# Convolution over 1563 fixed tiles of the sorted edge list, in chunks of 30, with a read base node and the radial attributes loaded by row

## The chip, the core and the metric

The program runs on one core of a Trainium2 chip. The metric is the time on the device in microseconds (us): the median of three runs of the whole program. The engines of the core are named PE (matmul; PEld is its weight load), DVE (vector), ACT (scalar), POOL and SP. POOL issues the gathers, SP most of the other DMAs. Each engine works through its own instructions in a fixed order and waits on semaphores for the others.

## What is computed

Two graph layers over 6250 nodes of 128 features and 200,000 edges that are sorted by their target `dst`. The first is a pair of attention layers with a residual; the change leaves it alone. The second is a convolution, and it is what the change is about:

```
h  = relu(layernorm(x))
f  = h @ W_lin_feat          # per node, 128 wide: 32 scalars, 32 vectors
s  = h @ W_lin_self
e  = f[src]                  # gathered per edge
w  = W_tp . gelu(gelu(edge_attr_8 @ W_mlp1) @ W_mlp2)   # 8 -> 64 -> 64 -> 4x32 per edge
m  = products of w, e and edge_attr_4 (a0, a1)          # 256 wide per edge
agg[dst] += m                # sum over the edges of a node
x  = x + cos * s + sin * (agg @ Wf)
```

(Scale factors are left out.)

## The kernel before

The program first runs the attention layers (to about 3030 us of the profiled execution), ending with `finish2`, which writes the node features `f` to a table in DRAM (`table3`) and leaves x + cos * s for all nodes in SBUF (`xt`). Then comes the convolution, written as one loop that is fully unrolled.

*Blocks and windows.* The nodes are cut into 49 blocks of 128. For each block, a window of 34 x 128 = 4352 edges of the sorted list is taken that starts at the block's first edge; that start is found on the chip and read into a register (`window_start`). An edge of the window that belongs to another block gets no place in the block's one-hot matrix and so adds nothing. A window has 34 tiles of 128 edges (K), worked on in groups of 8, 8, 8, 8 and 2 tiles (`GROUPS`): 245 groups, 1666 tiles.

*One group* (`convolve`). POOL issues one indirect DMA per tile that fetches 128 rows of `table3` (`gather`, L308) into one of six buffers `G`. PE transposes the group's radial attributes (L1165), ACT copies the result to SBUF as `a8t` (L1167), and PE multiplies it with a block-wise copy of `W_mlp1`, one matmul per pair of tiles (L1172). Two tiles of a pair share the 128 rows of the output, 64 hidden values each. ACT applies the first gelu (`hid1`, L1175), PE the second layer (L1177), ACT the second gelu (`hid2`, L1179), and PE the last product, one matmul per tile (L1185), into `big`. ACT scales the gathered rows by a0 (`g0`, L1196, one instruction per tile). DVE makes the products (L1198 to L1208). ACT and DVE split the results into a rounded half and its remainder (`halve`, L324 and L325), and DVE makes the one-hot matrices of the next group (`one_hot`, L317). At last PE adds each tile into the block's accumulator, a matmul with the one-hot matrix as its weights (the scatter, L1214). The accumulator is one PSUM bank (`whole`, a pool of one buffer).

*The end of a block.* ACT copies one half of the accumulator and DVE adds the other (`sums3`, L1244 and L1245). `finish3` transposes the sums on PE (L1224), ACT copies them (L1226), PE multiplies them with `Wf` (L1229), DVE adds the residual from `xt` (L1232, L1233), and SP stores 128 rows of the output (L1237).

*Order.* The code above is the order in which the work is written; a scheduler then sets each engine's order. It draws the front end of one group (L1165 to L1185) ahead of the scatter of the group before, so that PE works on two or three groups in turn. At a block's end, twelve of the next group's L1185 matmuls stand between the last scatter and the transposes of `finish3`.

After the loop stands a general path (`general3`) for lists that break the assumptions (too many edges in a window, or an unsorted list). A flag that is computed on the chip decides on it, and with these inputs it isn't taken.

Of the kernel before, what the change touches and what calls it, by code (L numbers as in the profile page):

```python
# [25 lines left out]
F32 = mybir.dt.float32  # L27
# [20 lines left out]
HS = 7  # L48
LAG = 5
# [12 lines left out]
def gnn_kernel(ctx: ExitStack, tc: tile.TileContext, x, src, dst, attr4, attr8,  # L62
               W1, al1, ar1, b1, W2, al2, ar2, b2,
               Wl0, Wl1, Ws0, Ws1, Wm1, Wm2, Wtp, Wf0, Wf1, out):
# [23 lines left out]
    NROW = (E - WCAP) // WSTEP + 1  # L88
    assert NB % HS == 0 and ROWT % WSEG == 0 and REST and HD == P // 2 and (E - WCAP) % WSTEP == 0

# [177 lines left out]
    srcw = const.tile([P, NB, K], I32, name="srcw")  # L268
    dstw = const.tile([P, NB, K], F32, name="dstw")
# [266 lines left out]
    table3 = dram.tile([NB * P, D], F32, name="table3")  # L536
    counts = [dram.tile([NQ, P, NB * QN], BF16, name=f"counts{b}") for b in range(NB)]
# [92 lines left out]
    wm1_sb = const.tile([SB * NRAD, NPR, 2 * HID], F32, name="wm1_sb")  # L630
    nc.vector.memset(wm1_sb, 0.0)
    for c in range(SB):
        nc.scalar.dma_start(wm1_sb[c * NRAD:(c + 1) * NRAD, c % NPR, c // NPR * HID:(c // NPR + 1) * HID], Wm1)
# [392 lines left out]
    xt = ctx.enter_context(tc.tile_pool(name="xt", bufs=1)).tile([P, NB, D], F32, name="xt")  # L1026

# [7 lines left out]
    with tc.tile_pool(name="att2", bufs=1) as pool, tc.tile_pool(name="dense", bufs=2) as dense, \  # L1035
# [8 lines left out]
        def finish2(b0, n):  # L1044
# [44 lines left out]
            nc.sync.dma_start(rows_of(table3, b0, n), t3[:, :n, :])  # L1089

# [3 lines left out]
        for b0 in range(0, NB, 2):  # L1094
# [8 lines left out]
            acc = big().rearrange("p (k a) c -> p k (a c)", k=2)  # L1103
            for h0 in range(0, NB, HS):
# [55 lines left out]
    def convolve(G, n, a0, a1, a8, acc, start, stop, oh, then=None):  # L1160
# [3 lines left out]
        pa = small()  # L1164
        nc.tensor.transpose(pa[:n * NRAD, :P], a8.rearrange("p c r -> p (c r)"), ident)  # L1165
        a8t = cw.tile([SB * NRAD, P], F32, name="a8t")
        nc.scalar.copy(a8t[:n * NRAD, :], pa[:n * NRAD, :P])  # L1167

        npr = min(n, NPR)
        ph = small()  # L1170
        for j in range(npr):
            nc.tensor.matmul(ph[:, j * P:(j + 1) * P], wm1_sb[:n * NRAD, j, :], a8t[:n * NRAD, :],  # L1172
                             start=True, stop=True)
# [39 lines left out]
        for c in range(n):  # L1213
            nc.tensor.matmul(acc, oh[:, c, :], ms[:, c].rearrange("e s h i u -> e (s h i u)"),  # L1214
                             start=start and c == 0, stop=stop and c == n - 1)
# [4 lines left out]
    def finish3(a, b, n):  # L1220
# [9 lines left out]
        o = cw.tile([P, D], F32, name="o")  # L1230
        xb = xt[:, ds(b, 1), :].rearrange("p o f -> p (o f)")
# [5 lines left out]
        nc.sync.dma_start(out[ds(b * P, n), :], o[:n, :])  # L1237

    with tc.tile_pool(name="conv", bufs=1) as pool, tc.tile_pool(name="gath3", bufs=6) as gath:
        again, some = flags(pool, over)  # L1240

# [6 lines left out]
        groups = [(b, *g) for b in range(NB) for g in GROUPS]  # L1248

        def hots(i):  # L1250
            b, s, n = groups[i]
            return one_hot(dstw[:, b, s:s + n], n)

        oh = hots(0)
        for i, (b, s, n) in enumerate(groups):
            if s == 0:
                r = window_start(b)
                a4 = cw.tile([P, K, 4], F32, name="a4", bufs=3)
                nc.sync.dma_start(a4, attr4[ds(r, CAP), :].rearrange("(p k) f -> p k f", p=P))
                a8 = cw.tile([P, K, NRAD], F32, name="a8", bufs=3)  # L1260
                nc.sync.dma_start(a8, attr8[ds(r, CAP), :].rearrange("(p k) f -> p k f", p=P))
                acc = whole()
                a1 = kept[:, P + b % 2 * 3 * K:P + (b % 2 + 1) * 3 * K].rearrange("p (k f) -> p k f", f=3)
                nc.vector.tensor_copy(a1, a4[:, :, 1:])
            cs = slice(s, s + n)
            G = gath.tile([P, SB, D], F32, tag="G", name="G")
            gather(G, table3, srcw[:, b, cs], n)
            oh = convolve(G, n, a4[:, cs, 0:1], a1[:, cs, :], a8[:, cs, :], acc, s == 0, s + n == K, oh,
                          (lambda i=i: hots(i + 1)) if i + 1 < len(groups) else None)
            if b and s == 0:  # L1270
                finish3(done, b - 1, P)
            if s + n == K:
                done = sums3(acc)
        finish3(done, FULL, REST)
# [4 lines left out]
        def general3(b, n):  # L1279
            with tc.If(flag_of(again[0:1, ds(b, 1)]) > 0):  # L1280
                nc.vector.tensor_copy(base, starts[:, ds(b, 1)])
                nc.vector.memset(tot3, 0.0)
                with tc.For_i(0, NCHUNK, 1) as i:
                    si, di = load_chunk(i)
                    dl = work.tile([P, GK], F32, name="dl")
                    nc.vector.tensor_scalar(dl, di, base, None, op0=OP.subtract)
                    at = []
                    for f, attr in ((4, attr4), (NRAD, attr8)):
                        t = cw.tile([P, GK, f], F32, name=f"a{f}g")
                        nc.vector.memset(t, 0.0)  # L1290
                        nc.sync.dma_start(t[:GP], attr[ds(i * (GP * GK), GP * GK), :].rearrange(
                            "(p k) f -> p k f", p=GP))
                        at.append(t)
# [40 lines left out]
```

## Time and profile before

| | us |
|---|---|
| median of three runs | 4724.91 |
| lowest, highest | 4715.71, 4729.55 |
| the profiled execution, its own time | 6136.95 |
| its span, first to last instruction | 6135.2 |

Busy time in the profiled execution, over the span:

| engine | busy us | share | instructions |
|---|---|---|---|
| PE | 3425.7 | 56% | 23441 |
| PEld | 2683.7 | 44% | 23442 |
| DVE | 3642.0 | 59% | 6107 |
| ACT | 2978.4 | 49% | 7370 |
| POOL | 2783.4 | 45% | 2787 |

The profiled execution is 30% longer than the timed ones; its durations of single instructions are used, and its waits have to be read with care. In the lines of the profile, a group is written as line, engine, operation, output<-inputs, shapes and count, then the busy time and the mean of one in ns, then the idle time of the engine just before these instructions and what ended it. "issue" is a wait for nothing that the profile shows, "remote" one that was ended from a queue it doesn't know. In the slices, each digit is a fortieth of the span, in tenths of busy time; PEclk is the granted clock of PE. In the order of time, a line has its start, its length, engine, line of code and operation.

### The profile page before, as it was taken

To read this page: it belongs to the slowest core of one execution; us is meant where nothing else is said; L and a number is where in the kernel's file an instruction comes from. 1 tells how busy PE (TensorE), PEld (TensorE's weight loads), DVE (VectorE), ACT (ScalarE), POOL (GpSimd) and SP (SyncE) were. 2 spreads that over 40 slices of the span, in tenths; PEclk is the share of its full clock that TensorE was granted. 3 is DMA by queue.
4 is the path that set the end of the run, shared out by engine and by line. 5 is a ranking of instruction groups with operands and counts; after the bars stand their busy time and mean duration, and the time that the engine had idled before them with its cause. 6 is when DMAs were issued, how large, how long until landed. Compare 5 with 4: busy or idle time off the path is not lost. (4 is left out here: it accounts for less than half of the span.)

```text
span 6135.2 us, 69889 instructions
## 1 busy us (share of the span) xinstructions
PE 3425.7 (56%) x23441; PEld 2683.7 (44%) x23442; DVE 3642.0 (59%) x6107; ACT 2978.4 (49%) x7370; POOL 2783.4 (45%) x2787
## 2 busy tenths in 40 slices
PE   3123555555555555799655555555655555655555
PEld 2013444454454444688534333333433333433333
DVE  4244655655665565788656565555655565556556
ACT  2012665665565566799634444334433433434434
POOL 1665545444544451000155555445555555545553
PEclk9999565666665566899867777667767667666667
DMA  3243434443443343444211111111111111111110
GB/s 86 63 115 85 119 111 115 117 115 111 125 123 113 108 129 122 171 163 154 89 42 42 40 40 41 38 40 40 42 41 42 40 41 41 39 38 42 39 40 25
DMA packets 338660, 480.00 MB, mean 78 GB/s; under 512 B 188987, under 2 KB 228555, under 8 KB 334306
## 3 DMA queue, kind: packets, MB, share of 16 engines
q1 hardware_dynamic: 186626, 232.52, 12.3%
q0 software_dynamic: 89072, 154.07, 10.7%
q10 hardware_dynamic: 62576, 88.69, 4.3%
q8 instruction: 191, 3.13, 0.2%
q14 instruction: 195, 1.60, 0.1%
HBM read 369.53 MB, written 105.48 MB: 77 GB/s over the span
## 5 line engine op out<-in xcount | busy, mean ns | idle before, releaser
L308 POOL DMA_INDIRECT G<-table,srcw x2720 | 2712.2, 997 | 2950.6 <-issue 989.7
L1214 PE MATMUL whole<-halves,ohr 128*128 128x512 f32 x1666 | 660.3, 556 | 255.6 <-DVE halves L325 228.1
L862 ACT ACTIVATE ramp<-erb,sel 128x256 bf16<-128x256 f32 x1764 | 758.4, 499 | 0.7 <-issue 0.3
L1177 PE MATMUL small<-hid,wm_sb 128*128 128x512 f32 (+1 forms) x490 | 335.3, 775 | 661.7 <-issue 467.2
L757 ACT CAST ca<-small 128x392 bf16<-128x392 f32 x784 | 349.3, 482 | 572.7 <-remote 383.5
L1214 PEld LDWEIGHTS whole<-halves,ohr 128*128 128x128 f32 x1666 | 433.9, 276 | 434.7 <-DVE halves L325 273.7
L325 DVE TENSOR_TENSOR halves<-mid,halves 128x1024 fp32r<-128x1024 f32 (+1 forms) x245 | 260.5, 1063 | 596.6 <-ACT halves L324 450.6
L1175 ACT ACTIVATE hid<-small 128x512 f32<-128x512 f32 (+1 forms) x245 | 135.6, 553 | 964.5 <-remote 579.4
L755 PE MATMUL small<-key,lo 128*128 128x98 bf16 x3136 | 333.5, 257 | 444.0 <-ACT ca L757 239.3
L1196 ACT ACTIVATE g<-G,a 128x128 f32<-128x128 f32 x1666 | 535.3, 394 | 17.9 <-DMA a<-in_edge_attr 8.3
L1185 PE MATMUL big<-wtp_sb,hid 64*128 64x128 f32 x3332 | 365.2, 356 | 221.7 <-issue 153.2
L1185 PEld LDWEIGHTS big<-wtp_sb,hid 64*128 64x128 f32 x3332 | 297.9, 247 | 412.3 <-issue 264.6
L1109 ACT ACTIVATE ramp<-small,sel 128x256 bf16<-128x256 f32 (+1 forms) x1225 | 447.8, 620 | 61.1 <-DVE up L1113 26.5
L755 PEld LDWEIGHTS <-lo 128*128 128x128 bf16 x3136 | 258.9, 127 | 481.6 <-issue 463.1
L325 DVE TENSOR_TENSOR halves<-big,halves 128x1024 fp32r<-128x1024 f32 (+1 forms) x245 | 259.3, 1058 | 354.2 <-ACT halves L324 175.9
L744 DVE TENSOR_TENSOR lo<-slots,turned 128x2048 bf16<-128x2048 bf16 x196 | 239.5, 1222 | 349.6 <-PE small L755 179.8
L1172 PE MATMUL small<-a8t,wm_sb 64*128 64x128 f32 (+1 forms) x1764 | 360.4, 355 | 96.4 <-issue 71.9
L882 PE MATMUL up<-rc,up 128*128 128x102 bf16 x3528 | 319.5, 264 | 165.9 <-DVE up L864 106.9
L1177 PEld LDWEIGHTS small<-hid,wm_sb 128*128 128x128 f32 x490 | 95.7, 241 | 719.5 <-issue 491.1
L1179 ACT ACTIVATE hid<-small 128x512 f32<-128x512 f32 (+1 forms) x245 | 135.8, 554 | 543.9 <-PE small L1177 284.1
L1172 PEld LDWEIGHTS small<-a8t,wm_sb 64*128 64x128 f32 (+1 forms) x1764 | 303.6, 251 | 169.9 <-issue 112.4
L370 PE MATMUL whole<-halves,ohr 128*128 128x136 f32 x1054 | 250.6, 387 | 218.3 <-issue 64.9
(273 smaller groups left out, 6596.2 us busy)
## 6 DMA issues: line engine op xcount, KB each, us to landing
counts<-ca ACTq DMA_DIRECT2D x196, 392.0 KB
ct<-counts SPq DMA_DIRECT2D x196, 392.0 KB
rc<-rhs SPq DMA_DIRECT2D x63, 717.5 KB
G<-table,srcw POOLq DMA_INDIRECT x2720
oht<-dlow SPq DMA_DIRECT2D x31, 1088.0 KB
ctc<-counts SPq DMA_DIRECT2D x504, 56.0 KB
a<-in_edge_attr SPq DMA_DIRECT2D x49, 136.0 KB
rhs<-rc SPq DMA_DIRECT2D x7, 717.5 KB
```

The costliest lines, as they stand in the source:

```text
L308: nc.gpsimd.indirect_dma_start(out=G[:, c, :], out_offset=None, in_=table, in_offset=bass.IndirectOffsetOnAxis(ap=idx[:, c:c + 1], axis=0))
L325: nc.vector.tensor_tensor(ms[1], m, ms[0], op=OP.subtract)
L755: nc.tensor.matmul(ps[:, k * NKEY:(k + 1) * NKEY], lo[:, a, :, r], ky[:, a, :, r], start=True, stop=True)
L757: nc.scalar.copy(ca[:, :, i * W:(i + WBANK) * W].rearrange("p h (k d) -> p h k d", d=W), ps[:, :WBANK * NKEY].rearrange("p (k h d) -> p h ...
L862: nc.scalar.activation(ramp[:, i, :n * P], erb[:, h, :n * P], AF.Relu, bias=sel1[:, h0 + i, h:h + 1], scale=STEEP)
L882: nc.tensor.matmul(ups[k][:, h], up[:, i, k * P:(k + 1) * P], by_head[:, i, :, h, :], start=h0 + i + h == 0, stop=h0 + i + h == NB + H1 - 2)
L1109: nc.scalar.activation(ramp[:, h, :n * P], pe[:, :n * P], AF.Relu, bias=sel2[:, h0 + h, :], scale=STEEP)
L1172: nc.tensor.matmul(ph[:, j * P:(j + 1) * P], wm1_sb[:n * NRAD, j, :], a8t[:n * NRAD, :], start=True, stop=True)
L1177: nc.tensor.matmul(ph[:, :npr * P], wm2_sb, hid1[:, :npr * P], start=True, stop=True)
L1185: nc.tensor.matmul(pw[:, c, :], hid2[half, j * P:(j + 1) * P], wtp_sb[half].rearrange("x p u -> x (p u)"), start=True, stop=True)
L1196: nc.scalar.activation(g0[:, c], G[:, c, :], AF.Copy, scale=a0[:, c, :])
L1214: nc.tensor.matmul(acc, oh[:, c, :], ms[:, c].rearrange("e s h i u -> e (s h i u)"), start=start and c == 0, stop=stop and c == n - 1)
```

## The change

The convolution no longer goes by blocks of nodes but by the edge list itself. The host cuts the list into 1563 tiles of 128 edges (the last one filled up) and hands it over as `src_tiles`, `dst_tiles`, `attr_4_tiles` and `attr_8_rows`, the last with one row per radial attribute. 195 groups have 8 tiles, one has 3.

The tiles are summed in 53 chunks of 30 (`CT`). A chunk has a base node, the target of its first edge, and its one-hot matrices count from there. `load_tiles`, called in the stage ahead of the convolution, reads the two lists, finds the bases, shifts `dst` by them and computes the flag for the general path (`again3`). At a chunk's end (`close`), which can fall within a group, the accumulator is read out as before. Since the next chunk's nodes overlap with it, its sums are carried over: `same`, a matrix that shifts rows by the difference of the bases, adds them into the next accumulator by one more matmul after six tiles. `finish3` then writes 128 rows at the base, and the next chunk overwrites those which it completes. Its residual rows come from a copy of `xt` in DRAM (`xtd`), loaded at the base, which SP reads from `base_i`.

For the first layer, the radial attributes are loaded by two DMAs per group straight into `a8t` (16 rows, 8 per half of the group, 512 columns; four buffers), so the transpose and the copy go, and one product of 512 columns takes the place of the four. `a4` is loaded for 40 tiles at a time.

```diff
+CT, LT = 30, 40
...
-    srcw = const.tile([P, NB, K], I32, name="srcw")
-    dstw = const.tile([P, NB, K], F32, name="dstw")
+    srcw = pool.tile([P, NB, K], I32, name="srcw")
+    dstw = pool.tile([P, NB, K], F32, name="dstw")
...
-    wm1_sb = const.tile([SB * NRAD, NPR, 2 * HID], F32, name="wm1_sb")
+    wm1_sb = const.tile([2 * NRAD, 2 * HID], F32, name="wm1_sb")
...
+    def load_tiles(pool):
+        nc.sync.dma_start(srcc, src_t)
+        raw = dstc.bitcast(I32)
+        nc.sync.dma_start(raw, dst_t)
+        firsts = pool.tile([1, NCH + 1], F32, name="firsts")
+        nc.vector.memset(firsts, N - 1.0)
+        nc.vector.tensor_copy(firsts[:, 1:NCH], raw[0:1, CT:NT:CT])
...
+        nc.vector.tensor_scalar(bd[:, 0, :], firsts[:, :NCH], float(N - P), None, op0=OP.min)
+        nc.vector.tensor_copy(base_i, bd[:, 0, :])
...
+        nc.vector.tensor_scalar(shift, ps[:, NCH:2 * NCH], -1.0, own, op0=OP.mult, op1=OP.add)
...
             nc.sync.dma_start(rows_of(table3, b0, n), t3[:, :n, :])
+            nc.sync.dma_start(rows_of(xtd, b0, n), xt[:, bs, :])
...
+            if b0 == 8:
+                load_tiles(pool)
...
-    def convolve(G, n, a0, a1, a8, acc, start, stop, oh, then=None):
-        pa = small()
-        nc.tensor.transpose(pa[:n * NRAD, :P], a8.rearrange("p c r -> p (c r)"), ident)
-        a8t = cw.tile([SB * NRAD, P], F32, name="a8t")
-        nc.scalar.copy(a8t[:n * NRAD, :], pa[:n * NRAD, :P])
+    def convolve(G, n, a0, a1, a8t, sink, oh, then=None):
         npr = min(n, NPR)
+        rows = NRAD if n <= NPR else 2 * NRAD
         ph = small()
-        for j in range(npr):
-            nc.tensor.matmul(ph[:, j * P:(j + 1) * P], wm1_sb[:n * NRAD, j, :], a8t[:n * NRAD, :],
-                             start=True, stop=True)
+        nc.tensor.matmul(ph[:, :npr * P], wm1_sb[:rows], a8t[:rows, :npr * P], start=True, stop=True)
...
         for c in range(n):
-            nc.tensor.matmul(acc, oh[:, c, :], ms[:, c].rearrange("e s h i u -> e (s h i u)"),
-                             start=start and c == 0, stop=stop and c == n - 1)
+            acc, start, stop = sink(c)
+            nc.tensor.matmul(acc, oh[:, c, :], ms[:, c].rearrange("e s h i u -> e (s h i u)"), start=start, stop=stop)
...
+        def close(c):
+            xb = cw.tile([P, D], F32, name="xb")
+            nc.sync.dma_start(xb, xtd[ds(first_node(c), P), :])
+            state["sums"] = sums3(state["acc"])
+            todo.append((c, state["sums"], xb))
+
+        def sink(t):
+            c, k = divmod(t, CT)
+            end = min(CT, NT - c * CT) - 1
+            if k == 0:
+                if c:
+                    close(c - 1)
+                state["acc"] = whole()
+            if k == min(6, end) and c:
+                same = cw.tile([P, P], F32, name="same")
+                nc.vector.tensor_scalar(same, slot, shift[:, c - 1:c], None, op0=OP.is_equal)
+                nc.tensor.matmul(state["acc"][:, :2 * D], same, state["sums"], start=False, stop=False)
+            return state["acc"], k == 0, k == end
...
+        for t in range(0, NT, SB):
+            n = min(SB, NT - t)
+            i = t // SB % (LT // SB)
+            if i == 0:
+                m = min(LT, NT - t)
+                a4 = cw.tile([P, LT, 4], F32, name="a4", bufs=3)
+                nc.sync.dma_start(a4[:, :m], attr4_t[:, t:t + m, :])
...
+            a8t = cw.tile([2 * NRAD, NPR * P], F32, name="a8t", bufs=4)
+            for j in range(2 if n > NPR else 1):
+                c = (t + j * NPR) * P
+                nc.sync.dma_start(a8t[j * NRAD:(j + 1) * NRAD, :], attr8_t[:, c:c + NPR * P])
...
+            gather(G, table3, srcc[:, t:t + n], n)
+            waiting = len(todo)
+            oh = convolve(G, n, a4[:, cs, 0:1], a1s[:, cs, :], a8t, lambda c: sink(t + c), oh,
+                          (lambda: hots(t + SB)) if t + SB < NT else None)
+            finish(len(todo) - waiting)
```

## The prediction, as put down before the changed kernel ran

> **What bounds the kernel now.** I read the time slices of the page first, then the busy time by stretch, then one block of the convolution in order of time, then the groups by shape and the waits.
>
> ```profile
> PE   3123555555555555799655555555655555655555
> POOL 1665545444544451000155555445555555545553
> PEclk9999565666665566899867777667767667666667
> ```
>
> From slice 20 on one even pattern runs to the end: the convolution. No engine passes six tenths, so nothing is full; the engines wait for each other.
>
> ```profile
> 3030.70:6135.20 3104.50, 1764.90 (x7791) 1187.18 (x7791) 1813.49 (x2648) 1236.82 (x2990) 1626.82 (x1666) 0.69 0.15 40
> 2485.00:3030.70 545.70, 489.31 (x5165) 450.66 (x5162) 460.24 (x855) 487.92 (x1350) 0.04 (x1) 0.98 0.40 140
> ```
>
> The columns are length, then PE, PEld, DVE, ACT, POOL busy, clock, DMA share, GB/s. The convolution takes 3104.5 us, 63.4 per block of 34 tiles, with the clock at 0.69; the stage ahead has it at 0.98 and PE nearly full.
>
> ```profile
> 4518.21 0.83 PE L1214 MATMUL whole<-halves,ohr 128*128 128x512 f32 x2
> ...
> 4525.87 2.07 PE L1172 MATMUL small<-a8t,wm_sb 64*128 64x128 f32 x8 [2.62 <-issue]
> 4533.32 2.07 PE L1177 MATMUL small<-hid,wm_sb 128*128 128x512 f32 x2 [5.38 <-issue]
> ...
> 4538.51 3.78 PE L1214 MATMUL whole<-halves,ohr 128*128 128x512 f32 x8
> ...
> 4548.34 2.13 PE L1214 MATMUL whole<-halves,ohr 128*128 128x512 f32 x8 [0.60 <-issue]
> ...
> 4556.39 1.22 PE L1177 MATMUL small<-hid,wm_sb 128*128 128x256 f32 x2 [1.18 <-ACT hid L1175]
> ...
> 4560.23 3.29 PE L1214 MATMUL whole<-halves,ohr 128*128 128x512 f32 x8
> ...
> 4570.71 3.78 PE L1214 MATMUL whole<-halves,ohr 128*128 128x512 f32 x8 [5.50 <-DVE halves L325]
> ...
> 4575.15 1.22 PE L1214 MATMUL whole<-halves,ohr 128*128 128x512 f32 x2
> ```
>
> L1214 is the scatter of one group. Its ends are 4519.04 (the pair that closes a block), then 4542.29, 4550.47, 4563.52, 4574.49, and 4576.37 for the next pair. So the first group of a block takes 23.25 us, the second 8.18, the third 13.05, the fourth 10.97, the pair 1.88. The third is late because the front end of the pair (its L1177 at 4556.39) stands ahead of it in PE's order.
>
> ```profile
> 4529.35 0.94 POOL L308 DMA_INDIRECT G<-table,srcw  x1 [0.30 <-issue]
> 4530.60 0.95 POOL L308 DMA_INDIRECT G<-table,srcw  x1 [0.30 <-issue]
> 4532.67 0.60 ACT L1175 ACTIVATE hid<-small 128x512 f32<-128x512 f32 x1 [5.91 <-remote]
> ```
>
> ```profile
> POOL G L308 <- ACT g L1196: 619.1, 80, 13.4
> PE small L1177 <- issue: 427.6, 81, 11.2
> ```
>
> One gather starts each 1.25 us, so 34 fill 42.5 of a block's 63.4 us. POOL waits 619 us for a gather buffer that ACT has to free: under the profiler it isn't the bound. 1666 x 1.25 = 2082 us is still a floor of the stage.
>
> ```profile
> L1177 PE MATMUL small<-hid,wm_sb 128*128 128x512 f32 x392 | 279.2, 801 | 505.8 <-issue 415.9 <-ACT hid L1175 89.9
> L1167 ACT COPY a8t<-small 64x128 f32<-64x128 f32 x196 | 49.2, 251 | 115.5 <-remote 61.2 <-PE small L1165 48.5 <-issue 2.5
> L1244 ACT COPY acc<-whole 128x256 f32<-128x256 f32 x49 | 18.3, 373 | 43.4 <-issue 29.9 <-PE whole L1214 13.4
> L1245 DVE TENSOR_TENSOR acc<-acc,whole 128x256 f32<-128x256 f32 x49 | 20.6, 421 | 38.4 <-ACT acc L1244 27.7 <-issue 10.5
> ```
>
> **What the Trainium skill says.** *Perfetto Trace Analysis*, section "Tensor Engine Instruction": the end of a matmul is computed from its size, not observed. The trace agrees: L1172 ends at 4527.94, yet ACT, which waits for it alone, starts at 4532.67. The same page, "GPSIMD Engine Instruction": take POOL's times from start to start; hence 1.25 us and not the 0.94 of the record. *TensorE: Matmul & The Clock Gate*, Part 1: PE falls to half its clock after an idle window of about 3.4 us. The clock of 0.69 beside waits of 5 us agrees. *DMA: Bandwidth & Descriptors*, "Latency and other measured facts": a DMA from SP needs 0.6 us to its first byte and some 2 us in all, which I use as an estimate for the new small loads; the trace shows no landing times.
>
> **The profiled execution and the timed ones.** The profiled one took 6136.95 us with a span of 6135.2; the median is 4724.91, 0.770 of it. The stage without gathers is already nearly full, so the excess must lie where engines wait. I make the sum on the profiled execution and scale it by 0.770. That is a choice: it assumes that the waits shrink alike.
>
> **The change part by part.**
>
> *Fewer tiles, no pairs.* 49 blocks of 8+8+8+8+2 tiles (1666) become 195 groups of 8 and one of 3 (1563). The 103 tiles are the 49 pairs and five more. A pair costs POOL 2 x 1.25 = 2.5 us. In the block shown it costs 4.87 (13.05 - 8.18) before its own scatter and 1.88 in it: 6.75. I take 6.5; the bounds are 2.5 and, if part of the first group's delay belongs to it too, 11.5. 49 x 6.5 = -318 us. The five tiles: 5 x 1.25 = -6.
>
> *More ends.* 53 chunks instead of 49 blocks: four more first groups. One takes 23.25 against about 9.1 for the others (8.18, 8.18, 10.97): 4 x 14.1 = +56.
>
> *The end now falls within a group.* There is one accumulator bank. PE's next scatter matmul waits for ACT's copy (0.373) and DVE's addition (0.421), about 0.9 with the handoffs; before, twelve L1185 matmuls filled that time. Behind the wait stand, on PE, the rest of the group's scatter, the two transposes and the product of the finish, then the next first layer; ACT and DVE wait for these. 52 x 0.9 = +47. Bounds: 0, if PE is waiting anyway, and 8 us each, if ACT's copy comes late behind eight scalings that wait for gathers.
>
> *The carry.* One fp32 matmul of 256 columns per chunk: half of an L1177 pair, which takes 1.12 to 2.08 us, so 0.56 to 1.04; 52 x 0.8 = +42. Its one-hot costs DVE about 0.25 x 52 = 13, hidden in DVE's idle time (DVE is busy 58% of the stage).
>
> *First layer.* Transpose, ACT copy and eight matmuls of 128 columns become one product of 512. The streaming is equal (L1172 x8 2.07 us, L1177 x2 2.07). What goes is a transpose (0.27 to 0.42), a copy (0.251) and their handoffs, about 1.0 us. It is on the path only at a chunk's end, where nothing else is interleaved: 53 x 1.0 = -53. Elsewhere it is hidden by the scatter of the previous group: nothing, or up to 1 us more per group without that cover.
>
> *Loads.* 391 loads of 8 x 2 KB and 53 of the residual rows go to SP's queue instead of 49 of a8. SP's order puts each first-layer load four groups (over 30 us) ahead of its use, behind the store of a finished chunk, which waits for DVE. At 2 us each they are hidden; the bound is a few us per chunk if that store is late. The stage ahead gains two lists of 800 KB and thirteen stores: 1.6 MB at its 140 GB/s is 11 us, beside its own loads; I take +5, bounds 0 and 15. The residual's addition, the store and the a1 copies (40 for 49) change nothing.
>
> Sum: -318 - 6 + 56 + 47 + 42 - 53 + 5 = -227. 6137 - 227 = 5910; times 0.770: 4550 us.
>
> **Rivals.** *POOL becomes the bound.* In the timed runs waits are short, the gathers' floor of 2082 us is near 0.770 x 3104 = 2390, and only 103 x 1.25 = 129 us go, unscaled: 4596. For it: the even 1.25 us. Against: POOL waits for buffers.
>
> *The late matmuls go too.* If the runs of short fp32 matmuls are what makes PE late, half of the 505.8 us ahead of L1177 goes as well: -477, so 5660 x 0.770 = 4358. For it: the wait follows eight L1172. Against: it may be the profiler's own.
>
> *Slower: the stop inside the group.* PE obeys its order; ACT's copy stands behind eight scalings of a later group, each waiting for its gather. If PE so loses 8 us more at each chunk's end, 52 x 8 = 416 - 227 = +189: 6326 x 0.770 = 4871. It decides from 227/52 = 4.4 us on. Against: before, the same copy stands behind the same scalings, and its row shows 43 us of idle time over 49 blocks.
>
> *The change doesn't do what it says.* If any chunk of 3840 sorted edges spanned over 128 nodes, the general path would walk the whole list 49 times, far beyond any range here. 32 edges per node make a span of 120, and a deviation of about 2 nodes leaves four of them as margin.
>
> **Numbers.** The forecast 0.50, POOL 0.17, the late matmuls 0.14, slower 0.14, the general path 0.01, the gain just given back 0.04. A measurement tells no change from one up to 0.3%, 14 us. Faster 0.81, same 0.04, slower 0.15. The range goes from the late matmuls' 4355 to 4740, leaving out the slower cases.
>
> **What would show it.** Right: some 196 groups, no 128x256 forms, about 9 to 11 us per group, the first of a chunk still above 20; L1214's idle time up by about 1 us per chunk; gathers 1.25 us apart. Wrong: waits of several us ahead of the first scatter after a chunk's end, PE waiting for the first-layer loads, or first groups above 30 us.

## The result and the profile after

| | median us | lowest to highest | runs |
|---|---|---|---|
| before | 4723.51 | 4715.71 to 4729.55 | 4 |
| after | 4649.91 | 4641.91 to 4653.88 | 4 |

The ratio is 0.9843 with an interval from 0.9823 to 0.9863: 74 us less (1.6%), where the prediction had 175. One thing has to be known for all that follows: these runs come from a chip on which the kernel before takes 4724 us, but all experiments below come from four other chips, on which the same kernel takes 6003 us or more. The profiled execution of before that the prediction was worked out on (6137 us) belongs to these by its time and by its waits, as round 2 shows; its chip is not on record. So each experiment is compared with before on its own chip, and the two kinds of chip are kept apart. The first kind was met only in these runs, and there is no trace of before from it. The profile of after is from the first kind: 4651.0 us, span 4649.3.

Its time slices, the three rows that were shown of before:

```profile
PE   3023676766667766399997678777777777777777
POOL 0677777666566665100002777777777777777774
PEclk9999766666666666599998676677677777766777
```

The convolution (from slice 22 on) has PE and POOL at seven tenths, where the page of before had PE at five to six and POOL at five. The same by stretch, the stage ahead and the convolution (length, then PE, PEld, DVE, ACT, POOL busy, clock, DMA share, GB/s):

```profile
1835.00:2525.40 690.40, 553.61 (x5776) 507.88 (x5776) 541.10 (x1009) 573.24 (x1568) 13.40 (x2) 0.90 0.44 153
2525.40:4649.30 2123.90, 1607.22 (x5895) 914.49 (x5895) 1675.20 (x2211) 1097.23 (x2454) 1592.78 (x1563) 0.71 0.22 57
```

2123.9 us instead of 3104.5, with DVE busy for 79% of it and PE for 76%. Most of this distance is the chip, not the change, as round 2 shows. One chunk's scatter in order of time:

```profile
4385.15 3.68 PE L1262 MATMUL whole<-halves,ohr 128*128 128x512 f32 x8 [3.28 <-DVE halves L332]
4393.47 2.07 PE L1262 MATMUL whole<-halves,ohr 128*128 128x512 f32 x4 [3.55 <-DVE halves L332]
4396.46 2.08 PE L1262 MATMUL whole<-halves,ohr 128*128 128x512 f32 x4 [0.92 <-DVE acc L1290]
4406.81 1.22 PE L1262 MATMUL whole<-halves,ohr 128*128 128x512 f32 x2
4408.33 3.12 PE L1262 MATMUL whole<-halves,ohr 128*128 128x512 f32 x6
4423.83 3.78 PE L1262 MATMUL whole<-halves,ohr 128*128 128x512 f32 x8
```

The chunk ends inside the group at 4393.47: four tiles, then 0.92 us for the read-out, then four tiles of the next chunk. The break after two tiles at 4408 is the carry. The waits of the whole convolution (time in all, times, longest):

```profile
POOL G L315 <- issue: 431.9, 1417, 0.3
PEld whole L1262 <- DVE halves L332: 392.5, 119, 5.7
PE whole L1262 <- DVE halves L332: 320.1, 93, 5.5
ACT hid L1222 <- PE small L1220: 313.7, 154, 7.6
...
PE whole L1262 <- DVE acc L1290: 42.0, 40, 4.2
```

Before, POOL waited up to 13.4 us for buffers and PE up to 11.2 us for nothing that the profile shows. Here POOL never waits more than 0.3 us once it has begun, so each gather simply follows the one before, 1.32 us from start to start on average. And the line of the read-out, beside the group of the first layer, whose matmuls waited for its loads only once, for 8.9 us:

```profile
L1220 PE MATMUL small<-a8t,wm_sb 16*128 16x512 f32 x392 | 294.3, 839 | 8.9 <-DMA a8t<-attr_rows 8.9
L1289 ACT COPY acc<-whole 128x256 f32<-128x256 f32 x53 | 19.7, 371 | 137.3 <-PE whole L1262 137.3
```

A POOL that never waits looks like the bound. It isn't, as the experiments show.

### The profile page after: what moved, and what is told of

Read it like the earlier page. It is cut to its first block, busy times and chain, and to the rows that moved or that the text cites. A ratio compares the mean times of both kernels' runs of the same rounds, so it can differ in the third digit from the quotient of the medians.

```text
span 4649.3 us, 65503 instructions
## 1 busy us (share of the span) xinstructions
PE 3221.1 (69%) x21547; PEld 2384.9 (51%) x21548; DVE 3499.3 (75%) x5685; ACT 2828.8 (61%) x6834; POOL 2785.6 (60%) x2684
## 3 DMA queue, kind: packets, MB, share of 16 engines
q0 software_dynamic: 85776, 147.31, 13.4%
## 5 line engine op out<-in xcount | busy, mean ns | idle before, releaser
L315 POOL DMA_INDIRECT G<-table,srcc x1563 | 1592.8, 1019 | 1027.5 <-DVE kept L1210 551.4
L315 POOL DMA_INDIRECT G<-table,srcw x1054 | 1121.0, 1064 | 568.2 <-issue 279.0
L1262 PEld LDWEIGHTS whole<-halves,ohr 128*128 128x128 f32 x1563 | 427.5, 288 | 607.6 <-DVE halves L332 392.5
L890 PEld LDWEIGHTS <-up 128*128 128x128 bf16 x3528 | 265.7, 129 | 183.4 <-DVE up L872 177.4
L332 DVE TENSOR_TENSOR halves<-big,halves 128x1024 fp32r<-128x1024 f32 x196 | 237.4, 1211 | 144.3 <-ACT halves L331 144.3
L872 DVE TENSOR_TENSOR up<-ramp,ctc 128x1792 bf16<-128x1792 bf16 x252 | 273.9, 1087 | 92.7 <-ACT ramp L870 71.3
L1224 PE MATMUL small<-hid,wm_sb 128*128 128x512 f32 x392 | 288.0, 825 | 74.4 <-ACT hid L1222 74.2
L377 PEld LDWEIGHTS whole<-halves,ohr 128*128 128x128 f32 x1054 | 217.3, 292 | 237.1 <-DVE halves L332 172.4
L1232 PE MATMUL big<-wtp_sb,hid 64*128 64x128 f32 x3126 | 307.4, 344 | 26.8 <-ACT hid L1226 26.8
L1222 ACT ACTIVATE hid<-small 128x512 f32<-128x512 f32 x196 | 116.8, 596 | 313.7 <-PE small L1220 313.7
L331 ACT CAST halves<-mid 128x1024 fp32r<-128x1024 f32 x196 | 204.1, 1041 | 160.9 <-DVE mid L1251 159.2
```

The source lines that it names most:

```text
L315: nc.gpsimd.indirect_dma_start(out=G[:, c, :], out_offset=None, in_=table, in_offset=bass.IndirectOffsetOnAxis(ap=idx[:, c:c + 1], axis=0))
L377: nc.tensor.matmul(acc, oh[:, c, :], ms[:, c].rearrange("e s f -> e (s f)"), start=start and c == 0, stop=stop and c == n - 1)
L872: nc.vector.tensor_tensor(up[:, :, :n * P].rearrange("p h (a d) -> p h a d", d=QN), ramp[:, :, :n * P].rearrange("p h (a d) -> p h a d", d ...
L890: nc.tensor.matmul(ups[k][:, h], up[:, i, k * P:(k + 1) * P], by_head[:, i, :, h, :], start=h0 + i + h == 0, stop=h0 + i + h == NB + H1 - 2)
L1224: nc.tensor.matmul(ph[:, :npr * P], wm2_sb, hid1[:, :npr * P], start=True, stop=True)
L1232: nc.tensor.matmul(pw[:, c, :], hid2[half, j * P:(j + 1) * P], wtp_sb[half].rearrange("x p u -> x (p u)"), start=True, stop=True)
```

## The experiments

**Round 1: the parts of the change.** Times in us; "ratio" is to before in the same round, whose median is in the last column.

| run | median | ratio, interval | before |
|---|---|---|---|
| e0_before | 6075.2 (one run) | | 6095.7 |
| e1_nopair | 5625.5 | 0.9242, 0.9201 to 0.9283 | 6095.7 |
| e2_nocarry | 5648.1 | 0.9268, 0.9225 to 0.9311 | 6095.7 |
| e4_ct24 | 5583.0 | 0.9171, 0.9131 to 0.921 | 6095.7 |

e0_before is the kernel before.

> The kernel before, profiled once more. If the long profiled execution (6137 us) was a disturbance of that one execution, as the changed kernel's own profile of 4651 us suggests, this one has a span near 4720 us and its waits are short. If the profiler stretches this kernel always, it is near 6100 us again.

e1_nopair is before without the closing pair of each block; the last two of 34 tiles are neither gathered nor summed:

```diff
-        groups = [(b, *g) for b in range(NB) for g in GROUPS]
+        groups = [(b, *g) for b in range(NB) for g in GROUPS[:4]]
...
-            oh = convolve(G, n, a4[:, cs, 0:1], a1[:, cs, :], a8[:, cs, :], acc, s == 0, s + n == K, oh,
+            oh = convolve(G, n, a4[:, cs, 0:1], a1[:, cs, :], a8[:, cs, :], acc, s == 0, s + n == 32, oh,
```

> The kernel before with the closing pair of each block left out of the convolution (two of 34 tiles are not summed), all else as it was. Theory 1, a pair costs only its gathers and its vector work (2.5 to 3.3 us): 120 to 165 us less than before, 4560 to 4605 us. Theory 2, the pair cost what the prediction took (6.5 us in the stretched profile, 5.0 scaled): 245 us less, 4480 us, and the change gives back some 170 us at its chunk ends.

e2_nocarry is after without the carry of a chunk's sums into the next:

```diff
-            if k == min(6, end) and c:
+            if False:
```

> The changed kernel without the carry (the one-hot of the shift and the matmul that adds the last chunk's sums are left out, so nodes that two chunks share are incomplete). Theory 1: the carry is about what was estimated, 0.6 to 0.8 us for each of 52 chunks, 4610 to 4620 us, or less if it is hidden. Theory 2, the ends of the chunks give the gain back and the carry is a large part of it: 2 us each or more, under 4550 us.

e4_ct24 is after with chunks of 24 tiles, so that each of its 66 ends lies between two groups:

```diff
-CT, LT = 30, 40
+CT, LT = 24, 40
```

> The changed kernel with chunks of 24 tiles instead of 30: 66 ends instead of 53, but each falls between two groups, so no scatter stands cut in two. Theory 2 (the stop within the group costs 2 us or more at three of four ends): the stop goes and the time falls below 4650 in spite of 13 more ends. Theory 1 (an end costs its chain of short steps wherever it falls, 4 to 6 us): 13 more ends add 50 to 80 us, 4700 to 4730 us.

e0 took 6075 us with the profiler, and the runs of before without it 6096, so the long execution is neither a disturbance of that one nor the profiler's doing. Leaving out the pair alone takes 470 us away, 9.6 us each. That was the first surprise: the change as a whole was worth only 74 in the result. The carry is worth nothing that can be measured (after itself has 0.9257 on this chip, in round 4), and ends between the groups bring something: e4 has 13 ends more than after and is still the fastest of the three. None of this fits 74 us; before takes 6.1 ms on this chip, and the next round put the changed kernel beside it on such a chip.

**Round 2: the changed kernel here, and both kernels with half the gathers.** In e7_half_before and e8_half_after, each second gather of the convolution is replaced by a plain load from SP of the table's first rows (so every second tile of 128 edges takes the features of those rows):

```diff
+    def gather_half(G, table, idx, n):
+        for c in range(0, n, 2):
+            gather(G[:, c:c + 1, :], table, idx[:, c:c + 1], 1)
+        if n > 1:
+            nc.sync.dma_start(G[:, 1:n:2, :], table[:n // 2 * P, :].rearrange("(c p) f -> p c f", p=P))
...
-            gather(G, table3, srcc[:, t:t + n], n)
+            gather_half(G, table3, srcc[:, t:t + n], n)
```

> The kernel before, looked at once more. The same kernel took 4724 us in the runs of the result and 6096 us in the last job, on another chip. If the chip decides, this look agrees within 1% with the time of the kernel before in this job; a span near 4720 us would show the convolution without late matmuls: some 2340 us, 47 to 48 us per block, POOL at 85 to 90% of its floor of 42.5 us.

> The changed kernel beside the kernel before on this chip. If the chip is like that of the result (4720 us before), the ratio is 0.984 again. If it is like that of the last job (6100 us before), theory A (late matmuls follow runs of many short fp32 matmuls, which the change cuts) expects a ratio of 0.92 to 0.94, theory B (late matmuls hit each kernel in the same measure) 0.98.

> The kernel before with each second gather of the convolution replaced by a plain load of the first rows of the table on SP's queue (those edges get the wrong rows). POOL's floor falls from 2082 to 1041 us. If POOL binds the convolution, the time falls by 100 us or more; if the block's chain binds it, by less than 30 us.

> The changed kernel with the same replacement. Theory POOL (the changed kernel's floor of 1563 x 1.25 = 1954 us is what holds it, at 1.25 of some 1.34 us per tile): it falls by 80 us or more and by more than the kernel before does. Theory chain: by less than 30 us.

| run | median | ratio, interval | before |
|---|---|---|---|
| e5_before | 6090.2 (one run) | | 6107.7 |
| e6_after | 5653.9 | 0.9257, 0.9228 to 0.9285 | 6107.7 |
| e7_half_before | 5232.6 | 0.8572, 0.8537 to 0.8606 | 6107.7 |
| e8_half_after | 5151.1 | 0.8449, 0.8412 to 0.8486 | 6107.7 |

On this chip the change brings 454 us, not 74. With half the gathers, the difference of the two kernels shrinks to 81 us. Both halved kernels lose far more than 100 us, which the expectations named as the sign that POOL holds the convolution; but before loses more than after (875 against 503 us), and the traces give another reason. This is before on a chip of the second kind (order of time, e13_look_before of round 4):

```profile
4078.07 1.16 PE L1172 MATMUL small<-a8t,wm_sb 64*128 64x128 f32 x8 [1.25 <-issue]
...
4079.14 0.94 POOL L308 DMA_INDIRECT G<-table,srcw  x1 [0.31 <-issue]
...
4087.87 0.94 POOL L308 DMA_INDIRECT G<-table,srcw  x1 [0.30 <-issue]
4088.30 0.60 ACT L1175 ACTIVATE hid<-small 128x512 f32<-128x512 f32 x1 [9.33 <-remote]
...
4088.95 2.07 PE L1177 MATMUL small<-hid,wm_sb 128*128 128x512 f32 x2 [9.72 <-issue]
```

PE's eight matmuls end at 4079.23 by their modelled time, and PE's semaphore, which ACT waits for, moves at 4088.27. POOL goes on meanwhile, and DVE until 4081.57. In the trace of after on the first kind of chip, a handoff of the same sort (second layer to second gelu) is immediate:

```profile
4380.75 1.12 PE L1224 MATMUL small<-hid,wm_sb 128*128 128x512 f32 x2
...
4381.91 0.60 ACT L1226 ACTIVATE hid<-small 128x512 f32<-128x512 f32 x1 [0.29 <-PE small L1224]
```

I counted in these traces where PE's semaphore moved more than 1 us after the modelled end of its last matmul. Such a place is called a stall of PE below. Some matmul records are missing from the traces, so the counts and sums are good to about a tenth, and sums under 100 us to some 10 us.

| trace | attention: stalls, us | convolution: stalls, us |
|---|---|---|
| after, chip of the result | 2, 10 | 1, 4 |
| before (e13_look_before) | 120, 413 | 200, 664 |
| after (e14_after) | 117, 471 | 65, 424 |
| before, half the gathers (e7) | 118, 413 | 46, 94 |
| after, half the gathers (e8) | 117, 440 | 12, 18 |

So PE stalls on the second kind of chip in the stages with gathers, and stalls in before add up to 1077 us, where 1379 us lie between 4724 and 6103; the rest isn't accounted for. Halving the gathers takes most of them out of the convolution: 570 us of the 875 that before loses, 406 of the 503 of after. That makes e7 and e8 a stand-in for the first kind of chip, and the changed kernel can be held against it. The stretch from 3200 to 4500 us, first after on the chip of the result, then e8_half_after (columns as above):

```profile
3200.00:4500.00 1300.00, 998.74 (x3657) 567.75 (x3656) 1041.00 (x1372) 677.80 (x1521) 1001.00 (x982) 0.71 0.22 58
```

```profile
3200.00:4500.00 1300.00, 995.98 (x3674) 567.28 (x3672) 1041.25 (x1369) 681.38 (x1528) 490.01 (x486) 0.72 0.21 58
```

All but POOL is equal, to 0.6% at most. The chunks also keep the same rhythm: in both traces their last scatters follow each other by 38.2, 47.4, 34.8 and 40.1 us in turn, 160.4 for four. POOL does half the work in one of them and nothing changes. Therefore the gathers' issue doesn't hold the convolution of after; POOL only keeps up with it, though it is close behind: 120 gathers at 1.32 us make 159 us. And if the stand-in is right for before too, its 2203.2 us from the first gather to the end, put behind the 2525.4 us at which the convolution begins in the trace of after, and 1.7 us around the span, give 4730 us. Measured: 4723.5. (That both kernels begin there together is taken from the other chips: 2982 to 3040 us in five traces of before, 3022 and 3031 in two of after.) For before this doesn't decide against POOL: 1.25 us a gather, and the 56 us by which some of its 1666 gathers last longer in the trace that the prediction used, make 43.6 us for 34, beside the 44.3 us per block of e7.

**Round 3: the parts again, on a third chip.**

> The kernel before, unchanged, for a trace beside the next three. Where the run takes about 4720 us: if the gathers' issue on POOL holds the convolution already (theory A), its 1666 gathers stand 1.27 to 1.32 us apart and POOL waits for no buffer there; if the closing pairs hold it still (theory B), the gathers stop for more than 3 us at the end of each of the 49 blocks, and their mean distance is 1.4 us or more. Where it takes about 6100 us, the distances of 1.80 us seen twice come again.

> The kernel before without the closing pair of each block (its two tiles are neither gathered nor summed): 98 gathers fewer. Where before takes about 4720 us: theory A (gathers' issue) gives 98 x 1.3 = 127 us less, about 4595, ratio 0.973; theory B (a pair costs 6.5 x 0.77 = 5 us and its gathers lie beside it) gives 49 x 5 = 245 less, about 4475, ratio 0.948. Where before takes 6100 us, 0.924 again.

> The changed kernel with the old first layer (attributes by node and transposed, one evacuation more, four products per group). If the gathers' issue holds the convolution (theory A), this work lies beside it: within 10 us of the changed kernel, ratio to before 0.984 to 0.987 where before takes about 4720 us. If the first layer stands in the chain as the prediction had it (theory B, 53 x 1.0 us x 0.77 = 41), 4690 us, ratio 0.993. Where before takes 6100 us the changed kernel stands at 0.926, and the two theories put this one at 0.926 and 0.934.

> The changed kernel with chunks of 24 tiles: 66 ends, all between groups, and none within one. If the gathers' issue alone holds it (theory A), 4640 to 4655 us where before takes about 4720, ratio 0.984. If an end within a group stops the gathers there (theory B: 26 chunks end within a group), it is 20 to 60 us less, ratio 0.972 to 0.98. Where before takes 6100 us, 0.917 again.

| run | median | ratio, interval | before |
|---|---|---|---|
| e9_before | 5958.8 (one run) | | 6002.8 |
| e10_nopair | 5684.5 | 0.9479, 0.943 to 0.9528 | 6002.8 |
| e11_oldfirst | 5645.2 | 0.9421, 0.9374 to 0.9468 | 6002.8 |
| e12_ct24 | 5521.2 | 0.92, 0.9149 to 0.9252 | 6002.8 |

e10 and e12 are the kernels e1 and e4 again. e11_oldfirst is after with the old first layer:

```diff
+        pa = small()
+        nc.tensor.transpose(pa[:n * NRAD, :P], a8.rearrange("p c r -> p (c r)"), ident)
+        a8t = cw.tile([SB * NRAD, P], F32, name="a8t")
+        nc.scalar.copy(a8t[:n * NRAD, :], pa[:n * NRAD, :P])
...
-        nc.tensor.matmul(ph[:, :npr * P], wm1_sb[:rows], a8t[:rows, :npr * P], start=True, stop=True)
+        for j in range(npr):
+            nc.tensor.matmul(ph[:, j * P:(j + 1) * P], wm1_sb[:n * NRAD, j, :], a8t[:n * NRAD, :],
+                             start=True, stop=True)
```

The chip was again of the second kind, and the expectations for it missed for e10 and e11: a pair costs 318 / 49 = 6.5 us here and 9.6 in round 1, so what it costs isn't the same from chip to chip. e12 came as expected (though 39 of the 52 ends of after lie within a group, not 26). In e9 the gathers stand 1.75 us apart, not 1.80. The ratio with the old first layer is 0.942, with the new one 0.926 on two other chips; as the same e1 and e10 differ by 0.024 between chips, this doesn't show which first layer is faster where PE stalls. The two were not run side by side there.

**Round 4: is it DVE that holds POOL?** In the trace of after, 177 of the 1563 gathers last over 1.2 us instead of 0.944. All of them begin while DVE runs the same instruction, and end 0.82 us after it:

```profile
2592.54 1.22 DVE L332 TENSOR_TENSOR halves<-mid,halves 128x1024 fp32r<-128x1024 f32 x1
2592.71 1.87 POOL L315 DMA_INDIRECT G<-table,srcc  x1 [0.31 <-issue]
```

It is the subtraction that makes the remainder of `mid`, and both its sources lie in SBUF. It is the only instruction of the loop on DVE of which that is true: the others with two sources have one in PSUM (`big`, `kept` or `whole`), and of the 863 gathers that begin during them none lasts over 0.953 us. If POOL were the bound, this would cost 118 us of the convolution and be the rest of the missing gain. (The expectations of rounds 3 and 4 still weigh that; that e8 keeps the rhythm of after was read from the traces only after them.) The edit gives the instruction one source in PSUM (`w` in place of the rounded half, so the remainder of `mid` is not what is summed); e16 has it in before:

```diff
-        halve([ms[:, :n, j, 1] for j in range(2)], m[:, :n])
+        nc.scalar.copy(ms[:, :n, 0, 1], m[:, :n])
+        nc.vector.tensor_tensor(ms[:, :n, 1, 1], m[:, :n], w, op=OP.subtract)
```

> The kernel before once more. Where it takes about 4720 us: gathers 1.27 to 1.30 us apart with about 60 us in gathers longer than 0.944 us (theory A, POOL holds the convolution already), or 1.4 us and more with stops at the ends of blocks (theory B). Where it takes about 6000 us: 1.75 to 1.83 us apart.

> The changed kernel, for comparison with the next two on one chip: ratio 0.984 where before takes 4720 us; 0.926 to 0.945 where it takes 6000 to 6100.

> The changed kernel, where the low half of the second message's rows is taken as mid minus w (in PSUM) instead of mid minus its own high half (in SBUF): the same instruction with one source in PSUM. If DVE's subtraction with two sources in SBUF holds off POOL's gathers (theory A), no gather of the convolution lasts over 1.2 us (177 in the trace of after, 81 in the earlier one at 5650 us) and their time over 0.944 us falls from 118 or 66 us to under 10; where before takes 4720 us the kernel is then 80 to 120 us faster than e14, where it takes 6000 us 0 to 60 us. If the long gathers come from transfers that collide (theory B), as many stay and the time is that of e14.

> The kernel before with the same one edit. Where before takes 4720 us, theory A (its convolution is held by POOL, with about 60 us of held-off gathers) gives 40 to 70 us less, theory B (held by the pairs) no more than 15. Where it takes 6000 us, 0 to 60 us less, and no long gathers left.

| run | median | ratio, interval | before |
|---|---|---|---|
| e13_look_before | 6097.7 (one run) | | 6102.8 |
| e14_after | 5636.5 | 0.9257, 0.9224 to 0.929 | 6102.8 |
| e15_psum_after | 5852.9 | 0.961, 0.9579 to 0.9641 | 6102.8 |
| e16_psum_before | 6050.0 | 0.9919, 0.989 to 0.9948 | 6102.8 |

The gathers' row in the answer on their line, for e14_after (count, then shortest, median and longest in ns):

```profile
L315 POOL DMA_INDIRECT G<-table,srcc x1563: 939/947/1987, 3021.5 to 5553.4; - x196
```

and for e15_psum_after:

```profile
L315 POOL DMA_INDIRECT G<-table,srcc x1563: 939/946/962, 3032.6 to 5794.5; - x196
```

That this instruction holds off the gathers is shown: no gather over 962 ns is left in e15, and none over 961 in e16, where e13_look_before has 73 over 1.2 us. What it is worth is not: e15 is 216 us slower than e14 where 0 to 60 less were expected; PE's stalls are 558 us instead of 424 there, 134 of the 216. Only e16 gained, 53 us. The edit also frees the subtraction from ACT's copy and so changes the order of the work; what makes e15 slower was not followed up.

**Round 5: the two disputed terms with few stalls.** Both kernels have half the gathers, by the edit of round 2, on e1_nopair and on e11_oldfirst.

> The kernel before without the closing pair of each block, and with every second gather of the convolution replaced by a plain load of the table's first rows. The same with the pairs has blocks of 44.3 us and 2203 us from the first gather of the convolution to the end. Theory A (the pair costs what its last matmuls come later there, 1.75 us): blocks of 42.5 us, 2203 - 86 = 2117 us. Theory B (the prediction's 6.5 x 0.77 = 5.0 us): 39.3 us and 1958 us.

> The changed kernel with the old first layer and every second gather of the convolution replaced by a plain load of the table's first rows. With the new first layer: 160.4 us per four chunks, 2122.5 us from the first gather of the convolution to the end, granted clock 0.71. Theory A (the first layer lies beside DVE's work there, and gains nothing): 155 to 163 us per four chunks, 2050 to 2150 us. Theory B (the prediction's 1.0 x 0.77 per group): 160.4 + 15 x 0.77 = 172 us, 2270 us at most; at least 2160. A gain of the old one would show as under 155 us, with a higher clock.

| kernel, half the gathers | first gather to end, us | rhythm, us | change from the line above |
|---|---|---|---|
| before (e7) | 2203.2 | 44.3 per block of 34 tiles | |
| without the pairs (e17) | 2035.4 | 40.7 per block of 32 | -168 |
| chunks, old first layer (e18) | 2052.5 | 38.6 per chunk of 30 | +17 |
| after (e8) | 2122.5 | 40.0 per chunk of 30 | +70 |

The whole programs took 5075.7 us (0.8335, 0.8293 to 0.8376) and 5069.7 (0.8322, 0.8281 to 0.8362), with before at 6087.6. e7 and e8 were run on one chip and e17 and e18 on another, so the table has the convolutions' lengths, and only the +17 lies within one chip. The stalls left in the four are 94, 128, 97 and 18 us, which makes the distances good to some tens of us; e18 is shorter than e8 in spite of its stalls. The pair costs 168 / 49 = 3.4 us, between the two theories. The first layer fell out on the side that neither theory had as its own: with the old one four chunks take 154.4 us on average, under 155 and with a higher clock, the sign that was named for a gain of the old form. The stretch 3200 to 4500 us in e18, to be held against that of e8 above:

```profile
3200.00:4500.00 1300.00, 946.30 (x4693) 649.92 (x4693) 1080.54 (x1429) 734.86 (x1714) 521.78 (x506) 0.78 0.21 60
```

PE is busy for less time although it does more of the work (1016 scatter matmuls against 976), and the granted clock is 0.78 against 0.72. In e7, on the chip of e8, it is 0.79:

```profile
3200.00:4500.00 1300.00, 937.73 (x4636) 629.10 (x4636) 1065.00 (x1574) 730.30 (x1773) 499.41 (x494) 0.79 0.21 57
```

In e17 it is 0.76, and in after 0.71, so in these five traces the low clock goes with the new first layer and not with the chip. Busy time by clock is 995.98 x 0.72 = 717 for 976 tiles and 946.30 x 0.78 = 738 for 1016: 0.73 per tile in both. The waits of e8 in this stretch:

```profile
PE whole L1268 <- DVE halves L338: 198.0, 57, 5.2
ACT hid L1228 <- PE small L1226: 189.1, 83, 7.6
```

and of e18:

```profile
PE whole L1273 <- DVE halves L338: 104.4, 42, 3.7
ACT hid L1233 <- PE small L1230: 102.3, 78, 2.9
```

The gelu behind the first layer waits up to 7.6 us for the new product and up to 2.9 for the old ones, and the scatter waits twice as long for DVE. The new loads are not what is late: in the whole of e8 PE waits for them once, 9.0 us. This fits a new product that often stands late in PE's order, but that is read from the waits alone. Whether the clock is the cause of the longer waits or follows from them stays open; no run separates them.

## Why the prediction was right in direction and wrong in size

The direction was right, and the time lies in the range; the gain was 74 us where 175 were forecast. Three steps failed above all: the scaling by 0.770, the price of the pair, and the first layer, which was given no cost. By its own steps:

**The scaling by 0.770.** It took the 6137 us of the profiled execution for the timed program with its waits stretched alike. The two numbers came from two kinds of chip. On one, PE stalls in the stages with gathers; on the other it doesn't, and the profiled run of after there takes as long as the timed ones. A stall doesn't shrink to 0.770 but to nothing, so one factor for all terms can't be right. The block that the terms were read from had such a stall in its first group, and so in the price of a further end: PE ends at 4527.94, ACT starts at 4532.67. I showed that line as proof that the modelled ends are wrong, and kept the wait in the price.

| term of the sum | predicted, then x 0.770 | measured, half the gathers |
|---|---|---|
| the pairs | -318, -245 | -168 |
| five tiles, ends, stop in the group, carry, loads | +144, +111 | +17 |
| first layer | -53, -41 | +70 |
| sum | -227, -175 | -81 (in the result -74) |

The right column is measured on the stand-in. That its sum fits the result doesn't show that each term is the same with all gathers: without the pairs, and with the old first layer, a tile takes 1.27 to 1.29 us there, less than the 1.32 us of a gather in the profile of after, so POOL could hold those two kernels.

**The pairs.** 6.5 us each met the chips with stalls (6.5 in round 3, 9.6 in round 1), in part by luck. With half the gathers it is 3.4, not 5.0: 77 us of gain less. Here it is not the stalls that failed but the way the price was read, as the third group's delay against the second. The settled blocks of e7, with few stalls, show the same: their groups end after 10.4, 8.3, 13.6 and 10.4 us, then 1.5 for the pair, and 13.6 - 8.3 + 1.5 is 6.8. But without the pair (e17) the groups take about 12.1, 10.6, 10.5 and 7.5 us: the first two are longer. A part of the time that the pair seemed to cost was only moved.

**The first layer.** The step reckoned that a transpose and a copy that go can only help, and gave no case in which the new product costs time. With half the gathers it costs 70 us, 111 away from the forecast, the largest miss. Equal streaming fits PE's work of 0.73 us per tile by clock; what differs are the waits for the new product and the clock. Which of the two comes first stays open.

**More ends.** 14.1 us for each further end was mostly the stall: in the blocks of e7 the first group takes 10.4 us, no longer than the last. In the trace of after, the first eight tiles of a chunk take 14 us on average, not over 20.

**The stop inside the group.** PE waits 42.0 us for the addition, 40 times, 1.05 each; 0.9 was forecast, but 52 times, where every fourth end lies between two groups. Ends, stop, carry, five tiles and loads together cost only 17 us in the stand-in, so most of such waits seem to replace others. The carry alone can't be measured: 0.9268 without it, 0.9257 with it, on the same chip. Chunks of 24, which end between groups, were faster than chunks of 30 where PE stalls: 0.9171 (0.9131 to 0.921) against 0.9257 (0.9224 to 0.929) on one chip, in rounds 1 and 4.

**What had to be seen.** 196 groups, no first or second layer of 256 columns, and 40.2 us per chunk or 10.7 per group came as forecast, and so did the read-out's wait. Gathers are 1.32 apart, not 1.25, because of DVE's subtraction.

**The rivals.** "POOL becomes the bound" has what looks like its sign in the profile of after, and falls with e8 for after; for before on the first kind of chip it stays untested. "The late matmuls go too" met the number on the chips with stalls: 5660 us unscaled, measured 5653.9 and 5636.5, and PE's stalls in the convolution go from 664 to 424 us, half of the gain. Its mechanism isn't shown: e11_oldfirst keeps the runs of short matmuls, and its stalls, by a like count, are 467 us, beside about 500 for before on that chip. The slower case and the general path didn't come.

Chunks with the old first layer may be better than after on the first kind of chip, but not by the whole 70 us: with all gathers at 1.32 us POOL needs 159 us for four chunks, against the 160.4 of after, which would leave some 20 us (an estimate from these numbers). It was run whole only where PE stalls, and no gain was seen there.

## What to carry to other kernels

When a profiled execution and the timed runs differ by a third, don't scale: find the waits that nothing explains (an engine's semaphore that moves long after its work has ended), take them out of the prices, and make the sum without them. The delay of one group against its neighbour isn't the price of the work in front of it: leave that work out and see what the neighbours do. An engine that never waits isn't shown to be the bound by that; halve its work and see whether the rhythm stays. And fewer instructions on PE is not yet a gain: look at where the new instruction stands in PE's order and at the granted clock of the stretch.

## What was not expected of the hardware

- The same kernel takes 4724 us on one chip and between 6003 and 6108 us on four others. On these PE's semaphore comes late in the stages with gathers, by the count of round 2 320 times in before and by up to 11.3 us at a time in its convolution (16 in that of after); with half the gathers, 46 places are left in the convolution instead of 200. What stops PE stays open, and so does what makes the one chip differ.
- A gather on POOL that starts while DVE runs a tensor-tensor instruction with both sources in SBUF lasts until 0.82 us after it, up to 1.99 us in e14_after instead of 0.944. The Trainium skill has this in *SBUF — State Buffer* ("Who interferes with whom"): such a DVE instruction contends with a GpSimd instruction that reads SBUF. The runs agree, if the gather, which takes its row numbers from SBUF, counts as one: 95 gathers over 1.2 us in e14, none of 1563 in e15, where one source lies in PSUM.
- The granted clock of a stretch was 0.72 with the new first layer and 0.78 with the old one, at the same matmul work per tile. The number of idle windows of 3.4 us, which the prediction took from *TensorE: Matmul & The Clock Gate*, Part 1, doesn't explain it: between 3200 and 4500 us PE has 25 longer ones in e8 (clock 0.72), 15 in e18 (0.78), 3 in e17 (0.76) and 30 in e7 (0.79). The clock goes down to half 76 times in this stretch of e17 and 89 times in that of e8, so most of these drops come without such a window.
